# A recurrent layer with side work: fixed units for the side steps, turns apart from their additions

## The chip, the cores and the metric

The kernel runs on one core of one Trainium2 chip. The metric is the time on the device of one execution in microseconds (us); a time is the median of several runs, and the profile is of one execution taken by the hardware profiler.

The core has five engines that run side by side, each through its own queue of instructions in order: TensorE (PE, matmuls; its weight loads are listed as PEld), VectorE (DVE), ScalarE (ACT), GpSimd (POOL) and SyncE (SP), which here only issues transfers. They wait for each other through semaphores. Matmul results land in PSUM banks, all else lies in SBUF, and large arrays in HBM.

## The reference

The input `x` has 128 sequences of 64 nodes with 256 features; `adj` is a 64 x 64 matrix of zeros and ones. Four layers follow, each wrapped as `x = layernorm(x + layer(x, adj))`, the norm over the 256 features. Layer 0 is a graph attention, layer 1 an attention over a list of 512 edges, layer 2 a graph convolution with two batch norms. The change is all in layer 3:

```python
h = relu(einsum('ts,bsh->bth', adj, x @ Wg0 + bg0))
h = relu(einsum('ts,bsh->bth', adj, h @ Wg1 + bg1))
for p in range(1, 5):
    nw = 64 // p
    wins = h[:, :nw * p, :].reshape(B * nw, p, 256)
    last = lstm_last(Wih[p-1], Whh[p-1], bih[p-1], bhh[p-1], wins)
    idx = arange(nw) * p + (p - 1)
    h = h.at[:, idx, :].set(last.reshape(B, nw, 256))
```

Two graph convolutions (the GCN) are followed by four small LSTMs with windows of p = 1, 2, 3 and 4 nodes. Each works on what the one before has written into `h`: the last node of each window is overwritten with the last hidden state. An LSTM step computes four gates (i, f, g, o) from the node's features and, from the second step on, from the hidden state.

## The kernel before

The 128 sequences of the last layer are done in eight groups g of 16 (`NG = 8`, `GB = 16`), one after the other. For each group there are three kinds of work.

`lstm(g)` is the main work. It is a generator that yields after each *unit*. A unit is one half j (128 of 256) of the hidden features of one step: 6 matmuls (three gates; the forget gate isn't needed in a first step) or 16 (four gates, input and hidden state), then the gates' sigmoid and tanh on ACT (L994), products on DVE (L997, L1001, L999) and GpSimd (L998), tanh of the cell on ACT (L1002), and after the second half the new hidden state, `hid` or, in the last step of a window, a write into the group's array `H` (L1011). A group has 22 units: units 0 to 3 for p = 1 and 4 to 7 for p = 2 (512 columns wide), 8 to 13 for p = 3 (336 columns), 14 to 21 for p = 4 (256 columns). `l` is the name of the PSUM tiles of the gates, of which there are five.

`gcn(g, half, ...)` prepares the `H` of a group, in two halves of eight sequences. It too is a generator. Its first part works on two pieces a: load `x2r` (the layer's input kept in HBM), scale the result of layer 2 that lies in `A` (L891, the second batch norm, on ACT), bring it from features-on-partitions to nodes-on-partitions, add (L896), normalise (`layernorm`) and store to `x3_dram`. Then the neighbours' sums (L878, 64 x 64 matmuls), the copies L914 and L915, the dense matmuls L921 with the bias L923 and relu L925, the matmuls L933 with L936, and sums again, written to `H` by L944 and L945. For group 0 the turning is done by PE transposes; for later groups by `turned`.

`turned(src)` turns a 128 x 512 tile without PE: DVE transposes its 32 x 32 blocks into a tile `st` (L860), SyncE stores that to HBM as `way` (L863), and loads it back block by block in four transfers into another `st` (L865). `st` tiles have five buffers, shared with other uses.

`final(g, s)` finishes the nodes t = s, s + 4, ... of a group: it gathers them (`hd`, copied by GpSimd in L1023), turns them, adds the layer's input `x3r` (L1036), normalises and stores to the output (L1045). Parts s = 0, 1, 2 can run when p = 4 begins, since p = 4 only writes the nodes of s = 3; s = 3 comes after the group's end. The very last one is done by PE transposes in two pieces.

Layernorm is two bn_stats and two bn_aggr on DVE, two small DVE operations, a power on GpSimd (L83) and the scaling (L97) on GpSimd.

The generators are interleaved in the program: while `lstm(g)` runs, after each unit some steps of the side work are recorded, the GCN of group g + 1 spread evenly over the units:

```python
        for u, _ in enumerate(lstm(g)):
            if u == 0 and g:
                final(g - 1, SKIP - 1)
            s, odd = divmod(u - first4, 2)
            if not odd and 0 <= s < SKIP - 1:
                final(g, s)
            while done < min(n_side, (u + 1) * n_side / (n_units - 2)):
                next(side, None)
```

The recorded order isn't the final one. A scheduler orders each engine's instructions by its own estimate of when each is ready, keeping dependencies; so a side instruction may be placed ahead of a unit's instructions on the same engine, or far ahead of the place at which it was recorded.

Of the kernel before, what the change touches and what calls it, by code (L numbers as in the profile page):

```python
# [8 lines left out]
F32 = mybir.dt.float32  # L9
# [8 lines left out]
P = 128  # L18
NB = 128
N = 64  # L20
D = 256
KD = D // P
# [6 lines left out]
QT = 512  # L29
# [5 lines left out]
SKIP = 4  # L35
# [6 lines left out]
def kernel(ctx: ExitStack, tc: tile.TileContext, i, out):  # L42
    nc = tc.nc
# [8 lines left out]
    A = main.tile([P, NQ, 2 * QT], F32, name="A")  # L52
# [3 lines left out]
    ident = const.tile([P, P], F32, name="ident")  # L56
# [55 lines left out]
    with ExitStack() as two:  # L112
# [5 lines left out]
        work = ph.enter_context(tc.tile_pool(name="work", bufs=2))  # L118
        ps = ph.enter_context(tc.tile_pool(name="ps", bufs=1, space=PSUM))

        def bank(shape, name="m", bufs=3):
            return (psm if name == "m" else ps).tile([P] + shape, F32, name=name, bufs=bufs)
# [612 lines left out]
        q = 0  # L735
# [90 lines left out]
    work = ctx.enter_context(tc.tile_pool(name="work3", bufs=2, reuse_waits="tile"))  # L826
# [7 lines left out]
    ST = 5  # L834
    TC = P // GB
    NG = NB // GB
    assert GB * N == 2 * QT

    def gbank(shape):
        return ps.tile([P] + shape, F32, name="g", bufs=3)  # L840
# [15 lines left out]
    def turned(src):  # L856


        t = work.tile([P, 4, 4, 32], F32, name="st", bufs=ST)
        nc.vector.transpose(t, src.rearrange("p n (j t) -> p j n t", t=32))  # L860
        o = work.tile([P, 4, 4, 32], F32, name="st", bufs=ST)
        way = dram.tile([P, 4, P], F32, name="way", bufs=4)
        nc.sync.dma_start(way, t.rearrange("p j n f -> p j (n f)"))  # L863
        for j in range(4):
            nc.sync.dma_start(o[j * 32:(j + 1) * 32].rearrange("t i n f -> t i (n f)"),  # L865
                              way[:, j, :].rearrange("(i t) x -> t i x", t=32))
        return o.rearrange("p i (c m) f -> p c m i f", m=KD)
# [14 lines left out]
    def gcn(g, half, bank, name):  # L882

        q = g * 2 + half
        for a in range(2):
            x = work.tile([P, 2, D], F32, name="x2r", bufs=4)
            nc.sync.dma_start(x.rearrange("p c d -> p (c d)"), x2_dram[q][:, a * 2 * D:(a + 1) * 2 * D])
            blk = A[:, q, a * QT:(a + 1) * QT]
            z = blk.rearrange("p (c m t) -> p c m t", c=2, m=KD)
            for m in range(KD):  # L890
                nc.scalar.activation(z[:, :, m, :], z[:, :, m, :], AF.Identity,  # L891
                                     bias=sh2[:, m:m + 1], scale=sc2[:, m:m + 1])
            if g:
                xt = turned(z.rearrange("p c m t -> p (c m) t"))
                xv = x.rearrange("p c (m i f) -> p c m i f", m=KD, f=32)
                nc.vector.tensor_add(xv, xt, xv)  # L896
            else:
                xt = bank([2, D])
                for m in range(KD):
                    for c in range(2):  # L900
                        nc.tensor.transpose(xt[:, c, m * P:(m + 1) * P], z[:, c, m, :], ident)
                nc.vector.tensor_add(x, xt, x)
            x3 = blk.rearrange("p (c d) -> p c d", c=2)
            layernorm(x3, x, 2, nc.gpsimd)
            for c in range(2):
                b0 = q * GQ + a * 4 + c * 2
                nc.sync.dma_start(x3_dram[b0:b0 + 2].rearrange("s t d -> (s t) d"), x3[:, c, :])
            yield

        x3 = A[:, q, :].rearrange("p (c d) -> p c d", c=PQ)  # L910
        p_ = neighbours(bank, lambda c, f: x3[:, c, f:f + 64])
        hT = work.tile([P, KD, QT], F32, name=name, bufs=2)
        dst = hT.rearrange("p k (c s n) -> p s (k c) n", c=PQ, s=2)
        nc.vector.tensor_copy(dst[:, 0], p_[0].rearrange("p k c n -> p (k c) n"))  # L914
        nc.scalar.activation(dst[:, 1], p_[1].rearrange("p k c n -> p (k c) n"), AF.Copy)  # L915
        yield
        hN = work.tile([P, KD, QT], F32, name=name, bufs=2)
        for m in range(KD):
            p_ = bank([PQ, P])
            for k in range(KD):  # L920
                nc.tensor.matmul(p_.rearrange("p c t -> p (c t)"), wg[0][:, k, m * P:(m + 1) * P], hT[:, k, :],  # L921
                                 start=k == 0, stop=k == KD - 1)
            nc.vector.tensor_add(hN[:, m, :].rearrange("p (c t) -> p c t", c=PQ), p_,  # L923
                                 rb[:, m:m + 1, :].to_broadcast([P, PQ, P]))
            nc.scalar.activation(hN[:, m, :], hN[:, m, :], AF.Relu)  # L925
            yield
        ys = []
        for a in range(2):
            p_ = bank([2, D])
            for c in range(2):  # L930
                t = (2 * a + c) * P
                for k in range(KD):
                    nc.tensor.matmul(p_[:, c, :], hN[:, k, t:t + P], wg[1][:, k, :],  # L933
                                     start=k == 0, stop=k == KD - 1)
            y = work.tile([P, 2, D], F32, name="st", bufs=ST)
            nc.vector.tensor_add(y, p_, bg1[:, None, :].to_broadcast([P, 2, D]))  # L936
            ys.append(y)
            yield
        p_ = neighbours(bank, lambda c, f: ys[c // 2][:, c % 2, f:f + 64])

        if g not in Hs:
            Hs[g] = work.tile([P, KD, N, GB], F32, name="H")
        dst = Hs[g].rearrange("p k t (h c s) -> p h s k c t", h=2, s=2)[:, half]
        nc.vector.tensor_scalar_max(dst[:, 0], p_[0], 0.0)  # L944
        nc.scalar.activation(dst[:, 1], p_[1], AF.Relu)  # L945
        yield

    GCN_STEPS = 8
# [67 lines left out]
    def final(g, s, pieces=1):  # L1016

        if s == SKIP - 1:
            h = lasts.pop(g)
        else:  # L1020
            h = work.tile([P, 2, KD, P], F32, name="hd", bufs=3)
            for c in range(2):
                nc.gpsimd.tensor_copy(h[:, c].rearrange("p k (w b) -> p k w b", b=GB),  # L1023
                                      Hs[g].rearrange("p k (c w s) b -> p c k w s b", c=2, s=SKIP)[:, c, :, :, s, :])

        rows = [v[g * GB:(g + 1) * GB].rearrange("b (c w s) d -> s c w b d", c=2, s=SKIP)[s]
                for v in (x3_dram, out_view)]
        xr = work.tile([P, 2, D], F32, name="x3r")
        for c in range(2):
            nc.sync.dma_start(xr[:, c, :], rows[0][c])  # L1030
        o = work.tile([P, 2, D], F32, name="st", bufs=ST)
        for cs in ([(0, 1)] if pieces == 1 else [(0,), (1,)]):
            r = slice(cs[0], cs[-1] + 1)
            if pieces == 1:
                xv = xr.rearrange("p c (m i f) -> p c m i f", m=KD, f=32)
                nc.vector.tensor_add(xv, turned(h.rearrange("p c m t -> p (c m) t")), xv)  # L1036
            else:
                ht = gbank([2, D])
                for c in cs:
                    for k in range(KD):  # L1040
                        nc.tensor.transpose(ht[:, c, k * P:(k + 1) * P], h[:, c, k], ident)
                nc.vector.tensor_add(xr[:, r], ht[:, r], xr[:, r])
            layernorm(o[:, r], xr[:, r], len(cs), nc.gpsimd)
            for c in cs:
                nc.sync.dma_start(rows[1][c], o[:, c, :])  # L1045

    def steps_of(g):

        if g:
            parts = [gcn(g, half, gbank, "hT") for half in range(2)]  # L1050
            order = [0, 0, 1, 1] + [0] * (GCN_STEPS - 2) + [1] * (GCN_STEPS - 2)
        else:
            parts = [gcn(g, 0, gbank, "hT"), gcn(g, 1, lbank, "hid")]
            order = [0, 0, 1, 1] + [0, 1] * (GCN_STEPS - 2)
        for half in order:
            next(parts[half])
            yield

    for _ in steps_of(0):
        pass  # L1060
    n_units = sum(-(-(N // p) // (QT // GB)) * p * KD for p in range(1, SKIP + 1))
    first4 = n_units - SKIP * KD
    for g in range(NG):

        side = steps_of(g + 1) if g + 1 < NG else iter(())
        n_side, done = 2 * GCN_STEPS, 0
        for u, _ in enumerate(lstm(g)):
            if u == 0 and g:
                final(g - 1, SKIP - 1)
            s, odd = divmod(u - first4, 2)  # L1070
            if not odd and 0 <= s < SKIP - 1:
                final(g, s)
            while done < min(n_side, (u + 1) * n_side / (n_units - 2)):
                next(side, None)
                done += 1
    final(NG - 1, SKIP - 1, pieces=2)


# [38 lines left out]
```

## Time and profile before

| | |
|---|---|
| time, median of 3 | 2156.92 us (2154.6 to 2158.59) |
| span of the profiled execution | 2156.5 us |
| PE busy | 2066.8 us (96% of the span) |
| PE weight loads busy | 1329.6 us (62%) |
| DVE busy | 881.6 us (41%) |
| ACT busy | 931.1 us (43%) |
| GpSimd busy | 418.7 us (19%) |
| first LSTM matmul starts | 814.42 us |
| last LSTM matmul starts | 2146.1 us |

The last layer's eight groups take 1332 of the 2157 us. The page of the profile has the engines' busy times, the costliest groups of instructions, and the chain of work that ended last; the trace behind it can be asked for the instructions of a stretch in order of time (the timeline), for busy times of stretches, and for who waited for whom. A line of the timeline has the start in us, the duration in us, the engine, the source line, the operation, the output and inputs, the shapes and the number of instructions merged; in brackets stand the idle time of that engine just ahead and what ended it. [...]

### The profile page before, as it was taken

How to read it: one execution, taken by the hardware profiler on the slowest of the kernel's cores; microseconds unless marked ns; L12 is line 12 of the kernel's file. 1: busy time of each engine (PE TensorE's matmuls, PEld its weight loads, DVE VectorE, ACT ScalarE, POOL GpSimd, SP SyncE). 2: the span in 40 equal slices, each digit the busy share in tenths (PEclk: the TensorE clock that was granted, in tenths of full speed). 3: DMA queues.
4: the chain of work that ended last, by engine and by line, in shares of the span. 5: the costliest groups of instructions: out<-in, count | busy, mean ns of one | idle time of the engine just before them, and what ended most of it. 6: DMA issues, size and time to landing. Idle time of an engine off the chain costs nothing.

```text
span 2156.5 us, 29415 instructions
## 1 busy us (share of the span) xinstructions
PE 2066.8 (96%) x11343; PEld 1329.6 (62%) x11343; DVE 881.6 (41%) x2069; ACT 931.1 (43%) x1795; POOL 418.7 (19%) x569
## 2 busy tenths in 40 slices
PE   5999999998999979999999999999999999999998
PEld 4666767665544444685576576577477478468466
DVE  7456665654444344233234233323323423423223
ACT  2776666664349064333334234334333333333332
POOL 1133334333200011021111111111111211202012
PEclk8999999999999979999999999999999999999999
DMA  5244531322240022012012112111201202202001
GB/s 154 51 68 80 85 58 48 53 40 43 44 123 20 0 88 79 1 55 81 22 50 69 40 34 64 59 29 55 74 11 59 88 6 60 72 1 59 20 3 56
DMA packets 232637, 113.42 MB, mean 53 GB/s; under 512 B 150192, under 2 KB 215728, under 8 KB 232240
## 3 DMA queue, kind: packets, MB, share of 16 engines
q1 hardware_dynamic: 230640, 109.57, 20.1%
q8 instruction: 89, 1.46, 0.3%
q0 software_dynamic: 1024, 1.05, 0.2%
q10 hardware_dynamic: 832, 0.92, 0.1%
q14 instruction: 52, 0.43, 0.1%
HBM read 67.45 MB, written 44.04 MB: 52 GB/s over the span
## 4 chain that ended last, share of the span: by engine, by line
PE 81%; DVE 7%; ACT 5%; DMA 3%; issue 2%; POOL 1%; SPq 0%; ACTq 0%; DVEq 0%; POOLq 0%
PE l L982 32%; PE l L988 19%; PE pz L719 5%; PE pz L784 4%; PE e L323 3%; PE g L921 2%; PE g L933 2%; PE m L295 2%; PE z L332 2%; PE m L298 2%; PE m L230 2%; PE g L878 1%; PE m L413 1%; DMA way<-st 1%; ACT A L891 1%
## 5 line engine op out<-in xcount | busy, mean ns | idle before, releaser
L982 PE MATMUL l<-H,wih 128*128 128x256 f32 (+2 forms) x2496 | 789.2, 471 | 11.3 <-DVE H L1011 6.1
L982 PEld LDWEIGHTS l<-H,wih 128*128 128x128 f32 x2496 | 469.9, 190 | 304.2 <-issue 188.7
L988 PE MATMUL l<-hid,whh 128*128 128x256 f32 (+2 forms) x1536 | 436.2, 437 | 1.2 <-DVE hid L1011 1.2
L988 PEld LDWEIGHTS l<-hid,whh 128*128 128x128 f32 x1536 | 291.8, 190 | 130.0 <-issue 61.2
L994 ACT ACTIVATE gate_i<-l,bias 128x256 f32<-128x256 f32 (+2 forms) x176 | 100.0, 568 | 515.1 <-PE l L988 440.3
L997 DVE TENSOR_TENSOR gate_i<-gate_i,gate_g 128x256 f32<-128x256 f32 (+2 forms) x96 | 48.4, 504 | 423.6 <-ACT gate_g L994 423.6
L998 POOL TENSOR_TENSOR cell<-gate_f,cell 128x256 f32<-128x256 f32 (+2 forms) x96 | 84.2, 877 | 666.1 <-ACT gate_f L994 666.1
L83 POOL TENSOR_TENSOR ln_rs<-ln_rs,mhalf 128x2 f32<-128x2 f32 (+2 forms) x97 | 78.0, 804 | 662.8 <-DVE ln_rs L95 662.5
L334 ACT ACTIVATE u<-z 128x1024 f32<-128x1024 f32 x128 | 130.3, 1025 | 64.3 <-PE z L332 63.3
L994 ACT ACTIVATE gate_g<-l,bias 128x256 f32<-128x256 f32 (+2 forms) x176 | 100.2, 569 | 100.3 <-PE l L982 52.0
L1002 ACT ACTIVATE gate_g<-cell 128x256 f32<-128x256 f32 (+2 forms) x176 | 90.0, 511 | 90.4 <-DVE cell L999 44.7
L994 ACT ACTIVATE gate_o<-l,bias 128x256 f32<-128x256 f32 (+2 forms) x176 | 99.2, 564 | 62.0 <-PE l L988 54.1
L719 PE MATMUL pz<-A,w 128*128 128x512 f32 x256 | 113.1, 595 | 0.0
L1001 DVE TENSOR_TENSOR cell<-gate_i,gate_g 128x512 f32<-128x512 f32 (+2 forms) x80 | 50.2, 627 | 142.5 <-ACT gate_g L994 142.3
L332 PE MATMUL z<-gath_r,qs 128*128 128x512 f32 x256 | 100.9, 482 | 0.6 <-ACT u L334 0.4
L306 DVE TENSOR_TENSOR qs<-m,qs 64x256 fp32r<-64x256 f32 x128 | 54.1, 422 | 109.0 <-ACT qs L305 106.9
L719 PEld LDWEIGHTS pz<-A,w 128*128 128x128 f32 x256 | 47.9, 190 | 55.4 <-issue 53.4
L295 PE MATMUL m<-wq,tT 128*128 128x260 f32 x256 | 72.5, 407 | 8.1 <-ACT yT L403 5.4
L994 ACT ACTIVATE gate_f<-l,bias 128x256 f32<-128x256 f32 (+2 forms) x96 | 51.0, 531 | 60.0 <-PE l L988 60.0
L1011 DVE TENSOR_TENSOR hid<-gate_o,gate_g 128x256 f32<-128x256 f32 (+2 forms) x96 | 48.4, 504 | 67.5 <-ACT gate_g L1002 39.5
L1011 DVE TENSOR_TENSOR H<-gate_o,gate_g 128x512 f32<-128x512 f32 (+1 forms) x64 | 40.9, 640 | 80.0 <-PE l L982 67.8
L721 DVE BATCH_NORM_STATS2 st<-pz 128x6 f32<-128x512 f32 x64 | 44.4, 697 | 59.5 <-PE pz L719 59.4
(242 smaller groups left out, 2518.4 us busy)
## 6 DMA issues: line engine op xcount, KB each, us to landing
way<-st SPq DMA_DIRECT2D x59, 256.0 KB
st<-way SPq DMA_DIRECT2D x236, 64.0 KB
xin<-in_x SPq DMA_DIRECT2D x16, 512.0 KB
ld<-table SPq DMA_DIRECT2D x16, 512.0 KB
x_dram<-y SPq DMA_DIRECT2D x16, 512.0 KB
x2r<-x_dram SPq DMA_DIRECT2D x32, 256.0 KB
x_dram<-A SPq DMA_DIRECT2D x64, 128.0 KB
x3r<-x_dram SPq DMA_DIRECT2D x64, 128.0 KB
```

The costliest lines, as they stand in the source:

```text
L83: nc.gpsimd.tensor_tensor(dst, dst, mhalf[:, :n], OP.pow)
L295: nc.tensor.matmul(pq, xT[:, k, c * P:(c + 1) * P], wq[:, k, :], start=k == 0, stop=k == KD - 1)
L332: nc.tensor.matmul(z[:, k, :], L1[q]["qs"][c][:, s, k * P:(k + 1) * P], gath_r, start=True, stop=True)
L334: nc.scalar.activation(u, z, AF.Relu)
L719: nc.tensor.matmul(p_, w1[:, k, m * P:(m + 1) * P], A[:, q, k * QT:(k + 1) * QT], start=k == 0, stop=k == KD - 1)
L784: nc.tensor.matmul(p_, w2[:, k, m * P:(m + 1) * P], hidden(q, k), start=k == 0, stop=k == M1 - 1)
L982: nc.tensor.matmul(gates[n], wih[p][:, k, mw * P:(mw + 1) * P], Hw[:, k, :, s, :], start=k == 0, stop=not s and k == KD - 1)
L988: nc.tensor.matmul(gates[n], whh[p][:, k, m * P:(m + 1) * P], hid[:, k], start=False, stop=k == KD - 1)
L994: nc.scalar.activation(act[n], gates[n], AF.Tanh if n == "g" else AF.Sigmoid, bias=bias[:, p - 1, m:m + 1])
L998: nc.gpsimd.tensor_tensor(cell[:, j], act["f"], cell[:, j], OP.mult)
L1002: nc.scalar.activation(act["g"], cell[:, j], AF.Tanh)
L1011: nc.vector.tensor_mul(Hw[:, jj, :, s, :] if over else new[:, jj], o, t)
```

## The change

Four things are changed, all in the last layer.

1. Each side step has a unit of its own, in a table, counted within the group that it runs beside. Half 0 of a GCN begins at unit 5 of the group before; half 1 begins seven units ahead of that group's start (units 15 and 16 of the one before it). For group 1, half 1 has its own row, since nothing runs ahead of group 0.
2. In later groups `gcn` is split: the loads, scalings and turns of both pieces come first (`fetch`), additions and norms are separate steps in later units (`norm`). `final` likewise yields between the turn and the addition: parts 0 to 2 add one unit later, part 3 two units later. A `final`'s output tile is taken only when it is needed.
3. What a unit's side steps put on ACT, DVE and GpSimd is queued behind the last instruction that was recorded for the unit on that engine (`tc.issue_after`). PE and SyncE aren't bound in this way.
4. GCN steps from the eighth on are recorded ahead of the other side steps of the same unit (`n < 7`).

What is computed stays the same. The aim is that side work no longer stands ahead of the LSTM's own instructions on an engine, and that a turn's way through HBM lies beside units and not in front of the addition.

```diff
     def gcn(g, half, bank, name):
         q = g * 2 + half
-        for a in range(2):
+        def fetch(a):
             x = work.tile([P, 2, D], F32, name="x2r", bufs=4)
             nc.sync.dma_start(x.rearrange("p c d -> p (c d)"), x2_dram[q][:, a * 2 * D:(a + 1) * 2 * D])
...
             if g:
-                xt = turned(z.rearrange("p c m t -> p (c m) t"))
-                xv = x.rearrange("p c (m i f) -> p c m i f", m=KD, f=32)
-                nc.vector.tensor_add(xv, xt, xv)
...
+                return x, turned(z.rearrange("p c m t -> p (c m) t"))
...
+        def norm(a, x, xt):
+            xv = x.rearrange("p c (m i f) -> p c m i f", m=KD, f=32) if g else x
+            nc.vector.tensor_add(xv, xt, xv)
...
             layernorm(x3, x, 2, nc.gpsimd)
...
+        if g:
+            came = []
+            for a in range(2):
+                came.append(fetch(a))
+                yield
+            for a in range(2):
+                norm(a, *came[a])
+                yield
+        else:
+            for a in range(2):
+                norm(a, *fetch(a))
+                yield
...
             if pieces == 1:
+                ht = turned(h.rearrange("p c m t -> p (c m) t"))
+                yield
                 xv = xr.rearrange("p c (m i f) -> p c m i f", m=KD, f=32)
-                nc.vector.tensor_add(xv, turned(h.rearrange("p c m t -> p (c m) t")), xv)
+                nc.vector.tensor_add(xv, ht, xv)
...
+    AT = [[5, 5, 6, 6, 7, 9, 9, 13, 13, 15], [-7, -6, -4, -2, 1, 3, 3, 7, 7, 11]]
+    AT1 = [0, 0, 1, 2, 3, 5, 5, 7, 7, 11]
+    side = {}
     for g in range(NG):
+        for half in range(2) if g else ():
+            part = gcn(g, half, gbank, "hT")
+            for n, u in enumerate(AT1 if half and g == 1 else AT[half]):
+                side.setdefault((g - 1) * n_units + u, []).append((n < 7, part))
+        for s in range(SKIP):
+            if g < NG - 1 or s < SKIP - 1:
+                part = final(g, s)
+                u = (g + 1) * n_units if s == SKIP - 1 else g * n_units + first4 + 2 * s
+                for v in (u, u + 1 + s // (SKIP - 1)):
+                    side.setdefault(v, []).append((True, part))
+    engines = (mybir.EngineType.Activation, mybir.EngineType.DVE, mybir.EngineType.Pool)
+    for g in range(NG):
         for u, _ in enumerate(lstm(g)):
-            if u == 0 and g:
-                final(g - 1, SKIP - 1)
-            s, odd = divmod(u - first4, 2)
-            if not odd and 0 <= s < SKIP - 1:
-                final(g, s)
-            while done < min(n_side, (u + 1) * n_side / (n_units - 2)):
-                next(side, None)
-                done += 1
-    final(NG - 1, SKIP - 1, pieces=2)
+            traced = nc.cur_bb.bb.instructions
+            with ExitStack() as order:
+                for e in engines:
+                    order.enter_context(tc.issue_after([t for t in traced[-300:] if t.engine == e][-1]))
+                for _, part in sorted(side.pop(g * n_units + u, []), key=lambda t: t[0]):
+                    next(part)
+    for _ in final(NG - 1, SKIP - 1, pieces=2):
+        pass
```

In the built program a second consequence can be seen: ahead of the first LSTM unit ACT has 8 of the scalings L891 (in the kernel before, all 64), and the rest stand after the units of their steps.

More of the change, by code (lines that the diff above doesn't have):

```diff
@@ L884, in gcn @@
         q = g * 2 + half
-        for a in range(2):
+        def fetch(a):
             x = work.tile([P, 2, D], F32, name="x2r", bufs=4)
             nc.sync.dma_start(x.rearrange("p c d -> p (c d)"), x2_dram[q][:, a * 2 * D:(a + 1) * 2 * D])
-            blk = A[:, q, a * QT:(a + 1) * QT]
-            z = blk.rearrange("p (c m t) -> p c m t", c=2, m=KD)
+            z = A[:, q, a * QT:(a + 1) * QT].rearrange("p (c m t) -> p c m t", c=2, m=KD)
             for m in range(KD):
@@ L893, in gcn @@
             if g:
-                xt = turned(z.rearrange("p c m t -> p (c m) t"))
-                xv = x.rearrange("p c (m i f) -> p c m i f", m=KD, f=32)
[L896 to L903, printed above, removed]
+                return x, turned(z.rearrange("p c m t -> p (c m) t"))
+            xt = bank([2, D])
+            for m in range(KD):
+                for c in range(2):
+                    nc.tensor.transpose(xt[:, c, m * P:(m + 1) * P], z[:, c, m, :], ident)
+            return x, xt
+        def norm(a, x, xt):
+            xv = x.rearrange("p c (m i f) -> p c m i f", m=KD, f=32) if g else x
+            nc.vector.tensor_add(xv, xt, xv)
+            x3 = A[:, q, a * QT:(a + 1) * QT].rearrange("p (c d) -> p c d", c=2)
             layernorm(x3, x, 2, nc.gpsimd)
@@ L907, in gcn @@
                 nc.sync.dma_start(x3_dram[b0:b0 + 2].rearrange("s t d -> (s t) d"), x3[:, c, :])
-            yield
+        if g:
[10 more added lines that the diff above has]
+                yield
         x3 = A[:, q, :].rearrange("p (c d) -> p c d", c=PQ)
@@ L1030, in final @@
             nc.sync.dma_start(xr[:, c, :], rows[0][c])
-        o = work.tile([P, 2, D], F32, name="st", bufs=ST)
         for cs in ([(0, 1)] if pieces == 1 else [(0,), (1,)]):
@@ L1042, in final @@
                 nc.vector.tensor_add(xr[:, r], ht[:, r], xr[:, r])
+            o = work.tile([P, 2, D], F32, name="st", bufs=ST)
             layernorm(o[:, r], xr[:, r], len(cs), nc.gpsimd)
@@ L1045, in final @@
                 nc.sync.dma_start(rows[1][c], o[:, c, :])
[L1047 to L1060, printed above, removed]
+        yield
@@ L1061 @@
+    parts = [gcn(0, 0, gbank, "hT"), gcn(0, 1, lbank, "hid")]
+    for half in [0, 0, 1, 1] + [0, 1] * (GCN_STEPS - 2):
+        next(parts[half])
     n_units = sum(-(-(N // p) // (QT // GB)) * p * KD for p in range(1, SKIP + 1))
     first4 = n_units - SKIP * KD
+    AT = [[5, 5, 6, 6, 7, 9, 9, 13, 13, 15], [-7, -6, -4, -2, 1, 3, 3, 7, 7, 11]]
+    AT1 = [0, 0, 1, 2, 3, 5, 5, 7, 7, 11]
+    side = {}
     for g in range(NG):
-        side = steps_of(g + 1) if g + 1 < NG else iter(())
-        n_side, done = 2 * GCN_STEPS, 0
```

## The prediction

> **What bounds the kernel now.** I read the page first (TensorE, PE, is busy for 96% of the span and is 81% of the chain that ended last), then the table of stretches of the last layer, then the chain and the timeline at the places where PE is not busy.
>
> ```profile
> core 0: us, PE busy (x) PEld busy (x) DVE busy (x) ACT busy (x) POOL busy (x), PEclk, DMA share, GB/s
> 980.00:1150.00 170.00, 167.18 (x808) 108.22 (x807) 57.80 (x132) 59.31 (x108) 27.95 (x42) 1.00 0.16 50
> ...
> 1320.00:1490.00 170.00, 169.12 (x814) 109.47 (x814) 58.67 (x134) 60.63 (x111) 28.68 (x43) 1.00 0.16 50
> ```
>
> From 814 us on, PE runs at full clock and the other engines are busy a third of the time. So only PE's holes can be won. How large are they? The chain gives the pace: `1152.40 13.75 PE l L982 x32`, so 0.430 us a record at 512 columns, and likewise 4.52/16 = 0.2825 at 336 and 3.45/16 = 0.216 at 256 (two records per matmul of the program). One group has 136, 152 and 216 such records: 58.4 + 42.9 + 46.6 = 147.9 us. The two halves of a later group's GCN put 18.2 us between them (each: 1.1 for either L878, 2 x 1.72 for L921, 2 x 1.73 for L933, by starts in the PE timeline). That makes 166.1 us. The first matmuls of the eight groups start at 814.42, 982.08, 1152.40, 1320.64, 1489.02, 1658.77, 1827.30 and 1996.00: periods of 167.66, 170.32, 168.24, 168.38, 169.75, 168.53 and 168.70. PE loses 1.6 us in the first group and 17.3 us in the next six.
>
> The timeline of group 1, where p = 1 hands over to p = 2, shows where:
>
> ```profile
> 1003.16 2.81 PE L982 MATMUL l<-H,wih 128*128 128x512 f32 x6 [0.48 <-ACT gate_g L1002]
> ...
> 1006.96 0.69 DVE L896 TENSOR_TENSOR x2r<-st,x2r 128x512 f32<-128x512 f32 x1 [3.95 <-DMA st<-way]
> 1007.57 0.68 DVE L1011 TENSOR_TENSOR H<-gate_o,gate_g 128x512 f32<-128x512 f32 x1
> ...
> 1008.31 4.13 PE L982 MATMUL l<-H,wih 128*128 128x512 f32 x9 [2.34 <-DVE H L1011]
> ```
>
> PE needs H of L1011; L1011 stands on VectorE (DVE) behind the addition L896, which waits 3.95 us for its turned tile to come back from HBM. 48 records end at 1002.7, 6 more take 2.6, and the next starts at 1008.31: 3.0 us lost. Even without that addition the hand-over costs something, as group 7 shows, which has no GCN beside it: 1996.00 + 48 x 0.43 = 2016.6, and H is written in full only at 2018.29.
>
> ```profile
> 2017.60 0.69 DVE L1011 TENSOR_TENSOR H<-gate_o,gate_g 128x512 f32<-128x512 f32 x1 [0.67 <-ACT gate_o L994]
> ```
>
> So some 1.8 us need filling by other PE work. The second hole lies ahead of the layer:
>
> ```profile
> 761.68 31.54 ACT L891 ACTIVATE A<-A,sh,sc 128x256 f32<-128x256 f32 x64 [64.63 <-DVE sh L704]
> ...
> 788.52 1.24 PE L878 MATMUL l<-bdT,A 64*64 64x64 f32 x32 [0.61 <-POOL A L97]
> ...
> 793.13 0.57 ACT L915 ACTIVATE hT<-g 128x512 f32<-128x512 f32 x1
> 793.61 0.58 ACT L915 ACTIVATE hid<-l 128x512 f32<-128x512 f32 x1
> 793.76 3.78 PE L921 MATMUL g<-hT,wg 128*128 128x512 f32 x4 [4.00 <-ACT hT L915]
> 797.33 2.93 PE L921 MATMUL l<-hid,wg 128*128 128x512 f32 x4
> ```
>
> The scheduler drew the 64 scalings L891 of all groups to the front of ScalarE (ACT); the copy L915, whose input PE had ready at about 786, waits behind them, and PE waits for it 4.0 us. The stretches table has PE's clock at 0.50 from 777 to 797 and at 1.00 from 800.
>
> **What the Trainium skill says.** "TensorE: Matmul & The Clock Gate", Architectural detail: ACT and DVE are strict FIFO. The trace agrees: L1011 starts when L896 ends. The same page, What's actually happening: idle PE falls to half clock, and a busy window of about 3.4 us brings it back. Here L921 runs at about half pace for some 5 us from 793.76, then at full. "DMA: Bandwidth & Descriptors", Rules for kernel authors: issue a transfer early and wait late; that is what the split of turn and addition does. "ScalarE: Activation LUTs", Table sets: identity, copy and relu are in every table set. The trace has Relu and Copy among the sigmoids with one table load at 813.78, and the built program has no more loads after the change than before, so scalings inside the layer cost no reload.
>
> **The change part by part.**
>
> *Scalings moved.* With every ACT part queued behind its unit, the built order has 8 scalings ahead of the layer instead of 64. The 56 others come after their units. At 0.49 us each (31.54/64) four add 2 us to ACT in a unit; ACT is busy for 35% and they stand after the unit's tanh, so PE hides them. Ahead of the layer, ACT is free when PE's L878 ends, at 786 and 789.76. L921 starts at 789.8 instead of 793.8: 4.0 us. PE then is busy from 788.5 and should be warm about 5 us later, so the first four L921 take 3.4 (half clock) and the next four about 1.8 to 3.4, ending at 795.0 to 796.6 instead of 800.26: 3.7 to 5.3, I take 4.9. The two transposes that stood among the H writes at 811 to 813 leave too; H is complete at about 813.9 instead of 814.32: 0.4. Sum 5.3.
>
> *GCN steps given units.* In the built order a later group has four L921 (3.44 us) between p = 1 and p = 2, eight L933 and a L878 (4.6 us) between p = 2 and p = 3, eight L933 (3.45 us) between p = 3 and p = 4. Each is longer than the 1.8 us to the H write, and their inputs come from units before, so the hand-over is filled.
>
> *Turn and addition apart.* A turn is 0.7 us of DVE transpose, then from the issue of way to that of st 2.05 us (1491.40 to 1493.45) up to 4.1 (997.85 to 1001.99, other transfers between), then to the addition 3.4 (1622.14 to 1625.51) up to 4.5 (1508.86 to 1513.34): 5.5 to 8.6 after the transpose. In p = 1 and 2 the additions stand at units 2 and 6, more than a unit of 5.2 or 13.7 us later. Where two are turned together (unit 5), the second waits in SyncE's queue behind the first (0.7 + 2.05 + 1.73 of issuing + 5.5 = 10, dear 0.7 + 4.1 + 1.7 + 8.6 = 15), against 13.7: at most 1.5 us of DVE waiting, with unit 7's products due 11 us later. Hidden.
>
> *The critical place is p = 4*, where five turns share SyncE's queue in 48 us and additions wait on DVE ahead of the next unit's product. Counted from the stage's start with the built order: final 0 is turned at 2.9, ready at 9.2 (12.3 at the dear price), its norm takes DVE to 12 (15); unit 16 needs DVE at 13.05 (PE starts it at 6.3, and 1612.42 to 1619.17 gives 6.75). Unit 16 writes no hidden state that PE waits for, and ACT's next gate is due at 17.9, so 2 us late costs nothing. Queued behind are: final 1, ready at about 25.5, DVE through at 27.1 against 26.85 due; the GCN's two, ready ahead of their additions; final 2 at 39.8, through at 41.7 against 40.65. Lateness of 0.3 to 1 us stays inside the ACT slack of 1 to 4 us.
>
> *So per later group* the period falls to 166.1 plus what small gaps remain. I leave 0.6 (0.1 to 0.2 at each L878, as in the trace now), 166.7: from 1013.9 us for six groups to 1000.2, a gain of 13.7.
>
> *Group 0 loses.* Its half 1 is turned only after unit 0 (before: ahead of the layer). The built order puts the second addition between the two H writes of unit 3 (0.4 us), and L878 after three matmuls of unit 4, before its norm on GpSimd is done: about 26.0 against 25.0. With no L921 ready to fill the hand-over, PE loses 2.5 to 3 and the period becomes 169.4: 1.7 us more than now.
>
> *Group 7 and the tail* have the same work as before; its hand-over keeps its 2 us. Sum: 5.3 + 13.7 - 1.7 = 17.3; 2156.9 - 17.3 = 2139.6.
>
> **Rivals.** *Half the gain.* SyncE's queue backs up (each way can only go once the out or x3 store ahead of it has its data), additions wait longer, and the groups keep about 1.2 us of holes each beyond my 0.6; the clock recovers late. For it: DVE waits 52.4 us for L1036 already now. Against it: none of those waits reaches PE in p = 4. 2139.6 + 7.2 + 1.6 = 2148.4. *Slower.* Turns in p = 4 take the dear price one after another (five times 3 us more), a DVE wait outlasts ACT's slack, banks of l come free late, and PE loses some 4 us in each of seven groups: 2139.6 + 28 = 2167.6. Against it: transfers are busy for only 16% of the time, and the dear price was seen where several transfers met. *Better.* PE is warm at once, group 0 loses nothing, gaps fall to 0.1: 2139.6 - 1.6 - 1.7 - 3.3 = 2133.
>
> **How the numbers follow.** Main case 0.66, half the gain 0.19, slower 0.06, better 0.09. The predicted time is the main case's, 2140. The range runs from just under the better case to above half the gain: 2132 to 2151. Beyond 0.2% (4.3 us) faster: main, half and better, less a little for a half gain that shrinks: 0.91; within: 0.03; slower: the slower case, 0.06.
>
> **What would show it.** Right: group starts 166 to 167 us apart; no PE wait on L1011's H in the middle groups; L915's successor at 786 and 789.8; the first LSTM matmul at about 809; DVE still waiting for st in p = 4. Wrong: PE waits on hid or on l's banks in p = 4, L878 waiting for GpSimd in later groups, or a layer start still near 814.

## The result, and the profile after

The changed kernel took 2138.20 us (median of 4 runs, 2138.01 to 2138.76), the kernel before 2157.68 beside it (2154.60 to 2158.59): a ratio of 0.9913, 95% interval 0.9895 to 0.9930, so 19 us faster. In the two profiled executions the span fell from 2156.5 to 2136.4, by 20.1 us.

Where the 20.1 us are, from the starts in the PE timelines:

| stretch | before | after | gain | predicted |
|---|---|---|---|---|
| up to the last L878 ahead of the first L921 (now L933): no code changed there | 788.52 | 787.49 | 1.0 | 0 |
| from there to the first LSTM matmul | 25.90 | 19.93 | 6.0 | 5.3 |
| group 0 | 167.50 | 168.57 | -1.1 | -1.7 |
| groups 1 to 6 | 1013.92 | 1001.14 | 12.8 | 13.7 |
| group 7 and the tail | 160.7 | 159.2 | 1.4 | 0 |

The prediction took the starts of the later groups from the chain, where they stand 0.16 us later than in the timeline (982.08 for 981.92), so it has 167.66 for group 0.

First the stretches of the last layer in the kernel after (columns as in the prediction: busy time of PE, PE's weight loads, DVE, ACT, POOL, each with its count; PE's clock; DMA share; GB/s).

```profile
980.00:1150.00 170.00, 170.00 (x817) 110.03 (x816) 59.34 (x134) 65.23 (x120) 29.66 (x42) 1.00 0.16 52
1320.00:1490.00 170.00, 170.00 (x878) 110.66 (x878) 59.95 (x135) 65.36 (x119) 29.80 (x42) 1.00 0.16 51
```

PE is busy for all of the 170 us, where it had 167.18 and 169.12. ACT shows some 5 us more: the scalings now run inside the layer, eight to a group, some 4 us (8 x 0.49). The periods of groups 1 to 6 are all 166.86, against 168.25 to 170.32.

The hand-over p = 1 to p = 2 of group 1, from the PE and the DVE timeline of the kernel after:

```profile
989.73 8.32 PE L994 MATMUL l<-H,wih 128*128 128x512 f32 x19
997.89 3.60 PE L933 MATMUL g<-hT,wg 128*128 128x512 f32 x8
1001.32 9.18 PE L994 MATMUL l<-H,wih 128*128 128x512 f32 x21
```

```profile
997.70 0.68 DVE L1023 TENSOR_TENSOR H<-gate_o,gate_g 128x512 f32<-128x512 f32 x1
999.06 0.69 DVE L1023 TENSOR_TENSOR H<-gate_o,gate_g 128x512 f32<-128x512 f32 x1 [0.68 <-ACT gate_o L1006]
```

Nothing stands between the two H products, H is complete at 999.75, and PE is with L933 until 1001.32. There is no bracket on any PE line: PE waits for nothing.

The start, PE and ACT timeline of the kernel after:

```profile
785.11 0.60 ACT L927 ACTIVATE hT<-g 128x512 f32<-128x512 f32 x1 [7.38 <-PE g L878]
788.89 0.60 ACT L927 ACTIVATE hid<-l 128x512 f32<-128x512 f32 x1 [3.18 <-PE l L878]
```

```profile
787.49 1.24 PE L878 MATMUL l<-bdT,A 64*64 64x64 f32 x32 [0.62 <-POOL A L97]
788.66 3.43 PE L933 MATMUL g<-hT,wg 128*128 128x512 f32 x4
791.93 1.88 PE L933 MATMUL l<-hid,wg 128*128 128x512 f32 x4
793.65 1.88 PE L933 MATMUL g<-hT,wg 128*128 128x512 f32 x4
```

The copies L927 now wait for PE (7.38 and 3.18 us), not PE for them; before, PE stood for 4.00 us at this place. The first four L933 take 3.27 us, the next 1.72: the clock is back near the end of the first tile. In the trace's record of the clock that PE was granted it is at half until 791.61, 4.1 us after the start of the last L878; in the kernel before it was at half until 799.43, 10.9 us after it.

What got worse is group 0, PE timeline:

```profile
828.22 0.69 PE L878 MATMUL g<-bdT,A 64*64 64x64 f32 x32
828.85 3.18 PE L994 MATMUL l<-H,wih 128*128 128x512 f32 x6
832.57 1.00 PE L878 MATMUL g<-bdT,A 64*64 64x64 f32 x32 [0.55 <-POOL A L97]
```

Here the second half of L878 waits for a norm (A, written on GpSimd) whose tile was turned only after unit 0. Six records of 0.43 end at 831.43, so 1.1 us are lost.

A gain that the prediction did not have is in group 7's p = 4. DVE and PE of the kernel before:

```profile
2132.43 0.69 DVE L1036 TENSOR_TENSOR x3r<-st,x3r 128x512 f32<-128x512 f32 x1 [5.57 <-DMA st<-way]
...
2135.80 0.42 DVE L1011 TENSOR_TENSOR hid<-gate_o,gate_g 128x256 f32<-128x256 f32 x1 [0.54 <-ACT gate_g L1002]
```

```profile
2136.28 3.29 PE L988 MATMUL l<-hid,whh 128*128 128x256 f32 x14 [1.21 <-DVE hid L1011]
```

and DVE of the kernel after, at the same place:

```profile
2113.66 0.43 DVE L1023 TENSOR_TENSOR hid<-gate_o,gate_g 128x256 f32<-128x256 f32 x1 [0.54 <-ACT gate_g L1014]
2117.14 0.69 DVE L1049 TENSOR_TENSOR x3r<-st,x3r 128x512 f32<-128x512 f32 x1 [3.05 <-DMA st<-way]
```

Before, the scheduler had drawn the final addition ahead of the product `hid` that ends the unit: `hid` came at 2136.2 and PE waited 1.21 us. After, the addition stands behind that product. For the turned tiles of `final` DVE waits no less (24 waits, 68.4 us in all, longest 4.8, against 16 and 52.4), but at places where nobody waits for DVE. For those of the GCN, 21 waits and 65.1 us before, it waits no more.

### The profile page after: what moved, and what is told of

Read it like the earlier page. It is cut to its first block, busy times and chain, and to the rows that moved or that the text cites. A ratio compares the mean times of both kernels' runs of the same rounds, so it can differ in the third digit from the quotient of the medians.

```text
span 2136.4 us, 29441 instructions
## 1 busy us (share of the span) xinstructions
PE 2060.7 (96%) x11343; PEld 1330.1 (62%) x11343; DVE 885.9 (41%) x2069; ACT 932.1 (44%) x1795; POOL 430.1 (20%) x569
## 4 chain that ended last, share of the span: by engine, by line
PE 86%; DVE 6%; ACT 4%; issue 2%; POOL 1%; DMA 1%; SPq 0%; POOLq 0%; DVEq 0%; ACTq 0%
PE l L994 36%; PE l L1000 20%; PE pz L784 5%; PE pz L719 5%; PE e L323 3%; PE g L933 2%; PE g L945 2%; PE m L295 2%; PE m L230 2%; PE z L332 2%; PE m L298 2%; PE g L878 1%; PE m L413 1%; PE m L270 1%; ACT u L334 1%
## 5 line engine op out<-in xcount | busy, mean ns | idle before, releaser
L1023 DVE TENSOR_TENSOR hid<-gate_o,gate_g 128x256 f32<-128x256 f32 (+2 forms) x96 | 47.4, 493 | 61.2 <-ACT gate_o L1006 35.1
L1023 DVE TENSOR_TENSOR H<-gate_o,gate_g 128x512 f32<-128x512 f32 (+1 forms) x64 | 41.3, 645 | 66.6 <-PE l L994 46.1
```

What stands on the lines that cost most here:

```text
L1023: nc.vector.tensor_mul(Hw[:, jj, :, s, :] if over else new[:, jj], o, t)
```

## The experiments

Each kernel was run beside the kernel before on the same chip, in five rounds. In the profiles I read four numbers: the start (last L878 ahead of the layer to the first LSTM matmul), group 0, groups 1 to 6 together, and the last group with the tail. The last L878 itself lies between 783.95 and 789.25 in these profiles, in code that no edit touches, so spans of two profiles are not compared directly. That point goes with the granted clock: up to 770 us PE was at half clock for 23.8 us in e13, 27.2 in e8, 30.7 in the kernel after and 34.0 in the kernel before, and the last L878 starts at 783.95, 785.71, 787.49 and 788.52.

| kernel | median (before beside it) | ratio, 95% | start | group 0 | groups 1-6 | last |
|---|---|---|---|---|---|---|
| before | 2157.68 | 1 | 25.90 | 167.50 | 1013.92 | 160.7 |
| after | 2138.20 (2157.68) | 0.9913 [0.9895, 0.9930] | 19.93 | 168.57 | 1001.14 | 159.2 |
| e3: before, ACT queued | 2154.02 (2160.00) | 0.9973 [0.9962, 0.9983] | 19.56 | 167.53 | 1016.1 | 160.9 |
| e4: before, all queued | 2162.64 (2160.00) | 1.0014 [1.0007, 1.0021] | 19.68 | 167.53 | 1028.9 | 159.2 |
| e13: before, split alone | 2160.79 (2156.59) | 1.0020 [1.0014, 1.0027] | 25.58 | 168.29 | 1018.6 | 161.1 |
| e2: after, nothing queued | 2146.24 (2160.00) | 0.9940 [0.9927, 0.9954] | 25.64 | 166.93 | 1002.2 | 160.2 |
| e9: after, only ACT queued | 2143.06 (2158.49) | 0.9930 [0.9917, 0.9943] | 19.80 | 168.56 | 1002.3 | 160.4 |
| e7: after, hand-overs not filled | 2146.91 (2160.00) | 0.9943 [0.9929, 0.9956] | 19.63 | 168.88 | 1007.1 | 159.2 |
| e5: after, GCN tiles not split | 2193.77 (2156.59) | 1.0167 [1.0145, 1.0190] | 19.93 | 175.30 | 1047.4 | 159.2 |
| e6: after, final tiles not split | 2138.06 (2156.59) | 0.9913 [0.9900, 0.9926] | 19.79 | 168.56 | 1001.1 | 159.2 |

**What the queueing does to the kernel before.** e3 and e4 wrap the calls of the side steps, which stay where they were:

```diff
+            traced = nc.cur_bb.bb.instructions
+            with ExitStack() as order:
+                for e in engines:
+                    order.enter_context(tc.issue_after([t for t in traced[-300:] if t.engine == e][-1]))
-            if u == 0 and g:
+                if u == 0 and g:
...
```

with `engines` only Activation in e3, and Activation, DVE and Pool in e4.

> The kernel before, with one addition: ScalarE's parts of the side steps are queued behind the unit's own; VectorE and GpSimd are ordered as before, and turn and addition stay in one unit. If the start's gain comes from the 56 scalings that no longer stand ahead of the copy, the first LSTM matmul comes some 6 us earlier (about 808) and the groups keep their periods (six groups about 1014): about 2151. Rival, that the earlier start is chance or belongs to the new units of the steps: the start stays near 814 and the time at 2157.

The start fell from 25.9 to 19.56 and the groups kept their periods but one. The 2.2 us more of groups 1 to 6 lie in group 4 (171.85 for 169.74): PE waits 0.6 us longer for H there (2.33 us, up to 1509.19), and its granted clock is at half from 1508.90 to 1512.31, which costs some 1.7 us more. So the start's 6 us come from the 56 scalings alone.

> The kernel before, with the parts of ScalarE, VectorE and GpSimd of the side steps queued behind the unit's own; units of the steps as before, turn and addition in one unit. In the built order both products that write H now stand ahead of the addition that waits for its turned tile, and PE still has nothing to put between p = 1 and p = 2. The theory of the prediction (the hand-over itself costs 1.8 us unless PE work fills it): periods of about 168.5, so 6 for the start and 3 for six groups: about 2148. Rival (only the addition ahead of the H product costs; the bare hand-over costs the 0.45 us of group 7): periods of about 167.3, so 6 and 10: about 2141.

Neither number came: it is slower than the kernel before. The start's 6 us are there, but groups 1 to 6 take 15.0 us more. PE and DVE timeline of e4, group 2:

```profile
1149.07 20.76 PE L982 MATMUL l<-H,wih 128*128 128x512 f32 x48
1170.32 10.54 PE L982 MATMUL l<-H,wih 128*128 128x512 f32 x24 [0.48 <-ACT gate_g L1002]
1180.78 0.69 PE L878 MATMUL g<-bdT,A 64*64 64x64 f32 x32
1183.13 1.00 PE L878 MATMUL g<-bdT,A 64*64 64x64 f32 x32 [1.65 <-POOL A L97]
```

```profile
1170.84 0.69 DVE L1011 TENSOR_TENSOR H<-gate_o,gate_g 128x512 f32<-128x512 f32 x1 [0.68 <-ACT gate_o L994]
1173.78 0.69 DVE L896 TENSOR_TENSOR x2r<-st,x2r 128x512 f32<-128x512 f32 x1 [2.24 <-DMA st<-way]
...
1178.56 0.68 DVE L896 TENSOR_TENSOR x2r<-st,x2r 128x512 f32<-128x512 f32 x1
```

The H products are free, as meant, and all that PE loses at the hand-over is 0.6 us (1170.32 - 1149.07 - 48 x 0.43). But the additions start 24.7 and 29.5 us after the group, where they started at 23.0 and 27.8, their norm comes later, and L878 of the next step now waits for it: 6 waits and 12.1 us in these groups, where the kernel before had none (its 2 waits, 3.5 us, lie ahead of the layer). And after these waits the clock falls to half. A stretch of e4 just after the second L878 above (columns as before):

```profile
1184.20:1187.50 3.30, 3.30 (x4) 1.31 (x5) 0.69 (x2) 0.60 (x1) 0.00 (x0) 0.50 0.54 183
```

In groups 1 to 6 there are four such stretches, 17.1 us in all, where the kernel before has none; at half pace they cost some 8.5 us. All waits of PE in these groups are 15.5 us against 8.9. That is 6.5 and 8.5 of the 15.0. Queueing without new units for the steps moved the wait from H to the norm, and made it longer.

**The split alone** (e13) puts the new `fetch` and `norm` into the kernel before, as four steps for each half where there were two:

```diff
-            order = [0, 0, 1, 1] + [0] * (GCN_STEPS - 2) + [1] * (GCN_STEPS - 2)
+            order = [0, 0, 1, 1] * 2 + [0] * (GCN_STEPS - 2) + [1] * (GCN_STEPS - 2)
...
-        n_side, done = 2 * GCN_STEPS, 0
+        n_side, done = 2 * GCN_STEPS + 4, 0
```

> The kernel before with the split alone: a later group's turn and its addition and norm are separate steps (four for each half instead of two, so 20 steps a group in place of 16), shared out over the units as before, nothing queued behind the unit's own. In the built order the 64 scalings and the addition between the two H products of p = 1 stand where they stood before. If a step's place in the program is nothing without its place in the queues: start at 814, six groups near 1014, same time as before: about 2158. Rival (the split by itself frees VectorE): six groups near 1006: about 2150.

As the first theory had it, and 0.2% slower. PE waits for H of L1023 6 times, 6.6 us, where it waited 6 times, 6.1 us: the scheduler draws a turned tile's addition ahead of the H product whether or not it is a step of its own. The split is not quite alone here: with 20 steps for 16, PE's parts of the GCN stand at other units too. By the starts of PE's records, e13 loses some 0.9 us a group (an estimate) at the hand-overs p = 2 to p = 3 and p = 3 to p = 4, where the kernel before loses nothing; that is most of the 4.7 us that its six groups are longer.

**The filled hand-overs.** e7 moves the steps that lie at units 3, 7 and 13 one unit forward:

```diff
-    AT = [[5, 5, 6, 6, 7, 9, 9, 13, 13, 15], [-7, -6, -4, -2, 1, 3, 3, 7, 7, 11]]
+    AT = [[5, 5, 6, 6, 7, 9, 9, 12, 12, 15], [-7, -6, -4, -2, 1, 2, 2, 6, 6, 11]]
```

> The kernel after, with half 1's steps at units 3 moved to 2 and those at 7 to 6, and half 0's at 13 moved to 12, so that no L933 stands between p = 1 and p = 2 and no L945 between p = 2 and 3 or 3 and 4. The theory of the prediction (1.8 us to be filled at the hand-over p = 1 to p = 2 of each later group): 6 x 1.8 = 11 us more than the kernel after: about 2149. Rival (a bare hand-over costs 0.45 us): about 3 us more: 2141.

Between the two: 0.98 us a group (167.84 for 166.86), 5.9 in six. The PE timeline of group 4 shows how little it is at each place:

```profile
1506.25 0.59 PE L945 MATMUL g<-wg,hT 128*128 128x256 f32 x2
1506.80 17.43 PE L994 MATMUL l<-H,wih 128*128 128x512 f32 x40
...
1548.88 0.83 PE L994 MATMUL l<-H,wih 128*128 128x336 f32 x2
1549.88 6.48 PE L994 MATMUL l<-H,wih 128*128 128x336 f32 x22 [0.17 <-DVE H L1023]
```

With one small L945 in place of eight records of L933, p = 2 starts without a wait. Its first records were not held up by the second H product, which ended at 1508.10 in this profile. p = 3 loses some 0.4 (1548.88 + 2 x 0.2825 = 1549.45, next at 1549.88) and p = 4 some 0.3 (24 records in 5.59 instead of 5.28 us). These two are no part of the 12.8 us that the change won, since the kernel before had work at both places already. Its PE timeline in group 3 (p = 3 begins at 1385.08, p = 4 at 1435.78):

```profile
1383.36 1.88 PE L921 MATMUL g<-hT,wg 128*128 128x512 f32 x4
...
1434.07 1.88 PE L921 MATMUL g<-hT,wg 128*128 128x512 f32 x4
```

So e7 measures what work at these places is worth, and leaves the hand-over p = 1 to p = 2 not quite bare.

**The queueing taken out of the kernel after** (`engines = ()` in e2, `engines = (mybir.EngineType.Activation,)` in e9).

> The kernel after, without the queueing of ScalarE, VectorE and GpSimd behind the unit's own: the units of the steps and the split of turn and addition stay. In the built order the 64 scalings stand ahead of the layer again, and in the later groups the addition stands between the two H products of p = 1 again, now with L933 on PE at that place. If units and split alone do the groups' part: six groups stay near 1001 and only the start's 6 us are lost: about 2144. Rival (the order of the queues does it): the additions block the H products again by 1 to 3 us a group, of which L933's 3.4 us may hide a part: 2148 to 2157.

Units and split do the groups' part: 1002.2 for six, and the start is back at 25.64. That is not because the additions kept away from the H products. DVE and PE of e2, group 4:

```profile
1503.28 0.68 DVE L1023 TENSOR_TENSOR H<-gate_o,gate_g 128x512 f32<-128x512 f32 x1
1505.48 0.69 DVE L902 TENSOR_TENSOR x2r<-st,x2r 128x512 f32<-128x512 f32 x1 [1.52 <-DMA st<-way]
...
1506.55 0.68 DVE L1023 TENSOR_TENSOR H<-gate_o,gate_g 128x512 f32<-128x512 f32 x1
```

```profile
1503.46 3.60 PE L933 MATMUL g<-hT,wg 128*128 128x512 f32 x8
1506.90 5.31 PE L994 MATMUL l<-H,wih 128*128 128x512 f32 x12
```

An addition stands between the H products, as in the kernel before, and H is complete only at 1507.2; but L933 fills PE until 1506.90, and PE's next records run on. The filling is what covers a blocked product.

> The kernel after, with ScalarE's parts alone queued behind the unit's own; VectorE's and GpSimd's are free. If only the scalings matter (the kernel with no queueing lost the start's 6 us and nothing in six groups): same as the kernel after, within 2 us: 2137 to 2140. Rival (VectorE's order is needed, since the turned additions may stand ahead of the H products again): 3 to 8 us more.

3.2 us more than the kernel after by the medians of the same chip (2143.06 and 2139.84), 2.4 in the profile: 1.2 in groups 1 to 6 and 1.2 in the last one, where PE stands 0.97 us for `hid` at 2116.96, as in the kernel before. The last column says the same of all kernels of the table: where DVE is queued it is 159.2, where it is not, 160.2 to 161.1.

**The split taken out of the kernel after.** e5 makes a GCN tile's turn in the unit of its norm; e6 makes a final tile's turn, addition and norm in one unit.

```diff
             for a in range(2):
-                came.append(fetch(a))
                 yield
             for a in range(2):
-                norm(a, *came[a])
+                norm(a, *fetch(a))
                 yield
```

> The kernel after, with the turn of a GCN tile made in the unit of its addition and norm again (units -4, -2 and twice 6), all else as it is: filling and queueing stay. If the split carries the gain: VectorE stands for 5.5 to 8.6 us at each of four places a group and the norms at unit 6 come late for L878 behind unit 7, where PE waits 2 to 3.5 us as it did in the kernel before with all three queues ordered; six groups 12 to 25 longer: 2150 to 2163. Rival (filling and queueing carry it, VectorE has slack for the wait): 0 to 3 us more than the kernel after: 2138 to 2141.

More than the first theory asked for: 46.2 us in six groups. PE waits for the norm (`PE g L878 <- POOL A L97`) 24 times, 32.0 us, of which 25.5 lie in these six groups. PE and DVE, group 4:

```profile
1518.61 0.46 PE L878 MATMUL g<-bdT,A 64*64 64x64 f32 x16 [1.09 <-POOL A L97]
1519.65 0.46 PE L878 MATMUL g<-bdT,A 64*64 64x64 f32 x16 [0.58 <-POOL A L97]
```

```profile
1514.78 0.69 DVE L902 TENSOR_TENSOR x2r<-st,x2r 128x512 f32<-128x512 f32 x1 [2.68 <-DMA st<-way]
...
1516.66 0.68 DVE L1012 TENSOR_TENSOR cell<-gate_i,gate_g 128x512 f32<-128x512 f32 x1
```

The turned tile comes so late that its addition keeps both waiting, the LSTM's own product L1012 that stands behind it on DVE, and L878, which needs the norm. Most of the rest is the clock. Right after these waits:

```profile
1520.20:1523.50 3.30, 3.30 (x4) 1.30 (x5) 0.66 (x1) 0.60 (x1) 0.00 (x0) 0.50 0.45 137
```

Records of 512 columns follow each other at 0.85 us here instead of 0.43. In groups 1 to 6 there are eight such stretches, 30.7 us in all, which cost some 15.4; with the 25.5 that is 40.9 of the 46.2, and 5.3 stay open.

```diff
                 ht = turned(h.rearrange("p c m t -> p (c m) t"))
-                yield
                 xv = xr.rearrange("p c (m i f) -> p c m i f", m=KD, f=32)
...
         yield
+        if pieces == 1:
+            yield
```

> The kernel after, with the turn of a final tile, its addition and its norm in one unit again, all else as it is. p = 4 has no other PE work to hide a late hidden state but one L878. If the waits for the turned tile reach PE there, as they did once in the last group of the kernel before (1.21 us): 1.2 to 3 us in each of eight groups, 10 to 20 in all: 2148 to 2158. Rival (ACT's slack of 1 to 4 us covers them, as the prediction reckoned for lateness up to 1 us): not over 2 us: about 2139.

The rival: the same periods to the digit (166.86), though DVE waits 64.4 us in 30 waits for final tiles. Queued behind the unit's own products, a final addition may wait; the split of `final` is worth nothing.

**Group 0 mended.** e8 takes group 1's second half out of the tables for its first two steps, as the kernel before had it:

```diff
-    AT1 = [0, 0, 1, 2, 3, 5, 5, 7, 7, 11]
+    AT1 = [0, 0, 2, 3, 3, 7, 7, 11]
...
             part = gcn(g, half, gbank, "hT")
+            if half and g == 1:
+                next(part), next(part)
...
-                side.setdefault((g - 1) * n_units + u, []).append((n < 7, part))
+                side.setdefault((g - 1) * n_units + u, []).append((n < (5 if half and g == 1 else 7), part))
```

> The kernel after, with group 1's second half scaled and turned ahead of the layer, as in the kernel before, and its later steps at the end of units 0, 0, 2, 3, 3, 7, 7 and 11, so that L933 fills the hand-over p = 1 to p = 2 of group 0 too. If group 0's 1.9 us over the others' period come from the late turn and the L878 that waits for its norm: period of group 0 about 167.0 instead of 168.7, 1 to 1.7 us less than the kernel after: about 2137. Rival (the four scalings and two transposes give it back ahead of the layer, 0.4 us or more at the H copy): not below 2138.

2135.85 us, a ratio of 0.9905 [0.9891, 0.9920]; group 0 took 166.93 instead of 168.57, the start 20.06. Since that was not beside the kernel after, both were then run on one chip, with e9 and with the edit and ACT alone queued:

> The kernel after as it is, for a comparison on the same chip with the three others: 2138, six groups 1001.1, group 0 168.7.

> The kernel with group 1's second half fetched ahead of the layer, once more, now beside the kernel after on the same chip. Group 0 took 166.9 instead of 168.7 in the first run, and the way from the last first-layer L878 to the first LSTM matmul 20.06 instead of 19.93: 1.7 us less than the kernel after. Rival (the difference of 2.3 us seen so far was drift from run to run): within 0.5 us of it.

> Both edits: group 1's second half fetched ahead of the layer, and ScalarE's parts alone queued. If the two are independent and VectorE's order is worth nothing: 1.7 us under the kernel after, about 2136. Rival: as much above the kernel with the fetch alone as the kernel with ScalarE's queueing alone stands above the kernel after.

2139.84 for the kernel after (0.9910 [0.9897, 0.9922]), 2137.38 for e15 (0.9908 [0.9895, 0.9920]), 2140.89 for e11 (0.9919 [0.9906, 0.9931]), 2143.06 for e9. The group 0 of e15 is again 166.93 against 168.58 (start 19.98 against 19.82), so the profile gives 1.5 us. The medians lie 2.5 us apart, but the intervals of the ratios overlap: the gain of group 0 is shown, a faster kernel is likely and not shown. The edit with ACT alone queued stands 3.5 us above e15 by the medians, as e9 stands 3.2 above the kernel after: no interaction of the two edits is seen.

## Why the prediction was right, and where it was not

The forecast was 2140 us and faster; the kernel took 2138.2. By its steps:

- **Scalings moved: right.** 4.0 us from L921 onwards and the clock back sooner: 5.4 up to the end of the second tile's matmuls (predicted 4.9, at most 5.3), H complete 0.55 earlier (0.4). e3 shows that ACT's queue alone does it, e2 that without it the start is as late as before (25.64). How soon the clock comes back is not quite set by the change: in the eleven profiles with ACT queued it was 3.1 to 4.2 us after the start of the last L878.
- **The period: right in size.** 166.86 where 166.7 was written. It was found as PE's work plus 0.6 us of small gaps, and measured it is the work plus 0.76.
- **GCN steps given units: the place right, the size wrong.** The step had it that "some 1.8 us need filling by other PE work" at p = 1 to p = 2, from the time between PE's last record and the second H product. PE does not need that product at once: six records of p = 2 run on the first one, as the prediction's own lines show. Group 7, with nothing to fill, loses 0.6 us there (1998.38 - 1977.14 - 48 x 0.43 in the kernel after). Counted over the first 54 records of a group, from the starts in the timeline, groups 1 to 6 of the kernel before lose 3.2, 1.1, 1.2, 2.6, 1.4 and 1.6 us at this place, 11.1 of the 12.8 won; the other 1.7 are smaller gaps elsewhere. In e4, where the H products are free and nothing fills, the same count gives 0.7 in each group. So, as an estimate, 4 of the 11.1 us are the bare hand-over and 7 the product behind a waiting addition. With L933 at the place both go, whatever stands between the products (e2). With the queues alone the 7 go, and more comes back as a wait for the norm and as time at half clock (e4).
- **Turn and addition apart: right for the GCN tiles and needless for the final ones.** e5 and e6 tell them apart: some 55 us by the ratios (1.0167 and 0.9913), and nothing. The prediction spoke of both in one. Much of the 55 is the clock at half after the waits, a cost that it did not have.
- **p = 4: right.** In group 4 the final additions start 9.21, 26.87 and 39.86 us after the stage (predicted ready 9.2, 25.5, 39.8), and unit 18's product comes at 28.35, 1.5 us after it was due: more than the 0.3 to 1 us reckoned, and still inside ACT's slack. PE waits for neither `hid` nor a bank.
- **Group 0: right in kind,** 1.1 us worse instead of 1.7, and by the step named (L878 ahead of its norm). e8 takes it back.
- **Group 7 and the tail: wrong.** "The same work as before" was true of the work and not of DVE's order. The prediction read group 7's hand-over and not its p = 4, where the list of PE's waits had `PE l L988 <- DVE hid L1011: 1.2, 1`. The 1.4 us come with DVE's queueing (the last column).

The 1.0 us ahead of the last L878 is no work of the change: it lies in code that is the same, and that point moved by 5 us among the profiles, with the time at half clock ahead of it.

Of the rivals, half the gain rested on gaps of 1.2 us more in each group; the gaps are not there. Slower was a step away: e5 differs from the kernel after in one place, and is 1.7% slower than the kernel before.

## What to carry to other kernels

Where PE is the bound, count its records and compare with the period before looking for a cause: that gave the gain of the groups to 1 us, while the hole to be filled was put at 1.8 us and measured 0.7. The parts of such a change don't add up. On the kernel before, queueing all three engines and splitting the steps each made it slower. Units and split together won the groups' part without any queueing (e2), and ACT's queue by itself the start (e3). Units without the split and without queues were not run. An instruction that waits for a transfer on an in-order queue costs PE time ahead of the unit's own product, unless other PE work covers it (e2). Behind the product it is harmless as long as its own result is not needed soon (e6), and dear where it is (e5). So ask for its place in the queue and for who needs its result, not for how long it waits. And a wait of PE can cost more than it lasts: in e4 the clock at half after the waits cost 8.5 us beside 12.1 of waits for the norm, in e5 15.4 beside 25.5.

## What the runs showed of the hardware

The Trainium skill's page "TensorE: Matmul & The Clock Gate" (What's actually happening) gives a busy window of about 3.4 us until the clock comes back, and calls the window free-running. The record of the granted clock agrees. The stretches at half clock among the groups of e3, e4 and e5 last 3.41 or 6.83 us, and those at the layer's start, in all 14 profiles, 13.7, 17.1, 20.5 or 23.9 us, whole multiples of 3.41. The time from PE's new start to full clock is not one window: after the hole of 4 us it was 5.7 us in the kernel before (793.76 to 799.43), 5.0 in e2 and 4.6 in e13. Where L933 (L921 in e3) follows L878 without that hole it was 4.1, 3.5 and 3.3 us from the start of the last L878 (the kernel after, e3, e8), although PE stood for 0.62 us just ahead of that. Whether the hole makes the difference, or only where the work fell in a window, no run here shows.

A hole shorter than a window can cost one. In group 4 of e3 the clock fell to half near the end of a wait of 2.33 us and stayed there for 3.41 us; after the waits of 1.09 and 0.58 us among the short L878 of e5 it did the same. The waits of 2.34 us in group 1 of the kernel before and of 2.29 in group 1 of e3 had no such cost.
